# A two-layer graph network on one core: the queries as seven block products, the softmax sums through a small DRAM table, the first layer norm in pairs of tiles

## The chip, the core and the metric

The kernel runs on one core of a Trainium2 chip. A core has TensorE (PE, matrix products into PSUM, with its weight loads shown as PEld), VectorE (DVE), ScalarE (ACT), GpSimd (POOL) and SyncE (SP, which only issues DMAs here). Each engine works through its own queue of instructions in order and waits for the others by semaphores. The metric is the device time of the whole kernel in microseconds, the median of several runs. All arithmetic is in float32.

## What is computed

There are B = 16 graphs of N = 1024 nodes with C = 256 channels; they share one adjacency matrix. The first layer mixes nodes by attention whose queries come from a weighted adjacency, the second is a graph convolution with two batch norms.

```python
# layer 0
h  = relu(layernorm(x))
c  = mean(h, axis=2)                                   # one number per node
A  = |(|sigmoid(c_j - c_i) - 0.5| - 0.5)| * 2          # symmetric
g  = relu((h^T @ (adj * A)) * para)                    # C x N, the queries
k, v = split(h @ kv_w)
x  = x + softmax(g_heads @ k^T * scale) @ v            # 4 heads of 64
# layer 1
h  = relu(layernorm(x))
An = adj + I;  dinv = rsqrt(rowsums + colsums - diagonal)
agg = (dinv_i * An_ij * dinv_j) @ h
y  = batchnorm(relu(batchnorm(agg @ W1^T + b1)) @ W2^T + b2)
x  = x + y
```

## The kernel before

A tile has 128 partitions. A graph has eight tiles of nodes (NT = 8) and two chunks of 128 channels (CC = 2); FB = 512 nodes is a half of the nodes[...]. The four heads are held as two channel chunks k with two heads each, so one *unit* of attention is (graph b, chunk k, half of the nodes f): 64 units.

The function `layers(False)` does everything up to the hidden layer of the second part; `layers(True)` and `second("s")` are a fallback that is skipped when the watched sums are in range. `second("f")` does the rest: hidden activations back from DRAM, batch norm, the product with W2, batch norm, residual.

**The foreground.** `attention()` (L806) walks 256 steps: each step is a quarter of a unit, two key tiles. `scores` (L696) makes four score products and two exponentials, `Unit.add` (L725) adds the exponentials up on VectorE in `acc`, `Unit.values` (L736) multiplies the previous step's exponentials with `v`. When a unit is through, `divide` (L756) sums `acc` over partitions by a product with ones (L762), takes 128x512 reciprocals in four pieces (L771), multiplies the output with them (L774), keeps their extremes (L777, L778), and two steps later `finish` (L792) transposes the output and adds it to `x` (L802).

**The background.** Between `values` and the next step's scores, `attention` draws *pieces* of about 1.7 us of TensorE from a generator, `background(b)` (L612), until the share that is due is done. The background of graph b prepares others: the weighted adjacency of graph b+1 (`weigh`, L363: abs and tanh on ScalarE, times adj on VectorE), its queries (`queries`, L407), its keys and values (`keys_values`, L441), the second layer norm of graph b-1, its aggregation over the graph (`aggregate`, L489) and hidden layer (`hidden`, L549), and for graph b+2 the norm, the broadcast of its node means (`differences`) and its transposes (`transposed`). `weave` runs several generators side by side, `soon` puts an action behind the next piece, and the marker `TOP` has a piece run between a step's scores and its values. Thus the program order, not a scheduler, decides what stands behind what on each engine.

**Queries before.** For each half q of the columns, two PSUM banks take the sum over eight node tiles: 16 pieces of four small matmuls per graph, 64 instructions and 128 records in a trace (a float32 matmul leaves two). The weights `w` live in four buffers.

**Aggregation.** It is already a block scheme of seven products instead of eight over 2x2 blocks (Strassen's idea in Winograd's form), with the blocks of the scaled adjacency made once by `graph()` (L221) during graph 1 and read from DRAM (`aht_d`) for each graph, three pieces ahead. Degrees are taken by `degrees()` (L203) during graph 0, from a second reading of the transposed adjacency.

**DMA queues.** SP issues all loads in program order: x, adj, para, aht, and the second layer's `yin` (L973). POOL issues the writes: x1, `y_d` (L565) from four `y` buffers, `aht_d`.

The first lines of the kernel's own order:

```python
norm = Norm(0, True)
run(norm.all())
differences(0, columns_of(csums[0], "c0"))
for k in range(CC):
    transposed(0, k)
run(weave(keys_values(0), (8 - AHEAD, islice(weighers[0], AHEAD))))
```

Of the kernel before, what the change touches and what calls it, by code (L numbers as in the profile page):

```python
# [17 lines left out]
P = 128  # L18
# [5 lines left out]
def gnn_two_layers_kernel(  # L24
# [36 lines left out]
    w2 = const.tile([P, HC, C], F32, name="w2")  # L61
# [4 lines left out]
    stats2 = const.tile([P, CC, B * NH, 6], F32, name="stats2")  # L66
# [6 lines left out]


# [10 lines left out]
    def layers(shifted):  # L85
# [12 lines left out]
        p3 = st.enter_context(tc.tile_pool(name=f"p3_{kind}", bufs=3))  # L98
        p4 = st.enter_context(tc.tile_pool(name=f"p4_{kind}", bufs=4))
# [41 lines left out]

        def bank(name):
            return ps_mm.tile([P, FB], F32, tag="mm", name=name)
# [15 lines left out]
        def load_adj(q, th, name):  # L159
            t = p4.tile([P, TH, FB], F32, tag="adj", name=name)  # L160
            nc.sync.dma_start(
                out=t,
                in_=adj[th * TH * P : (th + 1) * TH * P, q * FB : (q + 1) * FB].rearrange(
                    "(t p) m -> p t m", p=P
                ),
            )
            return t
# [4 lines left out]
        dbc = big.tile([P, N], F32, name="dbc")  # L172
        w1 = big.tile([P, CC, H1], F32, name="w1")
        rows = big.tile([P, NH, NT], F32, name="rows")

        def columns_of(col, name):

            cbs = []
            for g in range(NT // 4):
                cb = p2.tile([P, 4, P], F32, tag="cb", name=f"cb_{name}_{g}")  # L180
                nc.vector.tensor_copy(
                    cb, col[:, 4 * g : 4 * g + 4].unsqueeze(2).to_broadcast([P, 4, P])
                )
                cbs.append(cb)
# [10 lines left out]
        def load_adj_t(t, name):  # L195
            tile_ = p4.tile([P, N], F32, tag="adj", name=f"{name}_{t}")
# [3 lines left out]
        deg_sm = big.tile([P, 6, NT], F32, name="deg")  # L200
        row, diag, col, deg, tmp_deg, dinv = (deg_sm[:, i, :] for i in range(6))

        def degrees():  # L203

            nc.sync.dma_start(out=w1, in_=w1_t.rearrange("(k p) j -> p k j", p=P))
            nc.sync.dma_start(out=w2, in_=w2_t.rearrange("(k p) c -> p k c", p=P))
            nc.vector.tensor_reduce(row, rows.rearrange("p q t -> p t q"), AX.X, ALU.add)
            for t in range(NT):
                a = load_adj_t(t, "at")
                yield 0.0  # L210
                blk = a[:, t * P : (t + 1) * P]
                nc.scalar.activation(a, a, AF.Copy, accum_out=col[:, t : t + 1])
                db = p1.tile([P, P], F32, tag="db", name=f"db_{t}")
                nc.vector.tensor_mul(db, blk, ident)
                nc.vector.tensor_reduce(diag[:, t : t + 1], db, AX.X, ALU.add)
                yield 0.0
            nc.vector.tensor_add(deg, col, row)
            nc.vector.tensor_sub(deg, deg, diag)
            rsqrt(dinv, deg, 1.0, tmp_deg)

        def graph():  # L221


            HT, HB = NT // 2, FB // 2
            for t in range(HT):
                for part in range(2):
                    cols = slice(part * HB, (part + 1) * HB)
                    a = p4.tile([P, 2, NH, HB], F32, tag="adj", name=f"au_{t}_{part}")
# [6 lines left out]
                    for n in range(2):  # L235
                        if part == t * P // HB:
                            blk = a[:, n, n, t * P % HB : t * P % HB + P]
                            nc.vector.tensor_add(blk, blk, ident)
                        nc.vector.tensor_mul(
                            a[:, n], a[:, n], dbc.rearrange("p (m c) -> p m c", m=NH)[:, :, cols]  # L240
                        )
# [12 lines left out]
                    yield 0.0  # L254

# [87 lines left out]
        def transposed(b, k):  # L343

            h = hs["a", b]
            ht = p3.tile([P, N], F32, tag="ht", name=f"ht_{b}_{k}")
            hts.setdefault(b, []).append(ht)
            for g in range(NH):
# [14 lines left out]
        def weigh(b):  # L363
# [11 lines left out]
            for slot in range(2 * NH * NP + 1):  # L375
# [11 lines left out]
                if not odd and i < NH * NP:  # L387
# [3 lines left out]
                    w = p4.tile([P, TH, FB], F32, tag="w", name=f"w_{b}_{q}_{th}")  # L391
# [14 lines left out]

        def queries(b):  # L407

# [32 lines left out]
        def keys_values(b):  # L441
            ht = hts[b]
            ks[b] = [p4.tile([P, N], F32, tag="k", name=f"k_{b}_{k}") for k in range(CC)]
            for j in range(CC):
                for g in range(NH):
# [28 lines left out]
        def quarters(b):  # L474


            h = hs["b", b]
            HT = NT // 2
            return [h[:, n * HT : (n + 1) * HT, c * P : (c + 1) * P] for c in (0, 1) for n in (0, 1)]

        def combine(b):


            a11, a12, a21, a22 = quarters(b)
            s1s[b] = p1.tile([P, NT // 2, P], F32, tag="s1", name=f"s1_{b}")
            nc.vector.tensor_add(s1s[b], a21, a22)
            nc.vector.tensor_sub(a21, a11, a21)

        def aggregate(b):  # L489
# [5 lines left out]
            def load(upto):  # L495
                while len(pieces) <= min(upto, 7 * NP // 2 - 1):
                    i, th = divmod(len(pieces), NP // 2)
                    i = order[i]
                    a = p4.tile([P, TH, FB], F32, tag="adj", name=f"aht_{b}_{i}_{th}")
# [3 lines left out]
            load(2)  # L503
            yield 0.0
            a11, a12, a21, a22 = quarters(b)
            s1 = s1s[b]
# [4 lines left out]
            add, sub = nc.vector.tensor_add, nc.vector.tensor_sub  # L511

# [4 lines left out]
            def second(m):  # L517
                add(c11, m, c12)
                sub(a12, a12, a11)

            def fifth(m):
                add(c22, m, c21)
                add(c12, m, c12)

            for i, (left, after) in enumerate(
# [6 lines left out]
                    (a22, lambda m: add(c21, m, c21)),  # L532
                    (a12, lambda m: add(c12, m, c12)),
# [3 lines left out]
                for th in range(NP // 2):  # L537
                    n = i * NP // 2 + th
                    load(n + 3)
# [35 lines left out]
        def normed(b):  # L575
# [3 lines left out]
            combine(b)  # L579
# [4 lines left out]
        def normed_last():  # L584
# [6 lines left out]
            combine(B - 1)  # L591
            nc.gpsimd.dma_start(out=x1_d[B - 1], in_=xs[B - 1])

        def prepare(b, products):
# [8 lines left out]
            for k in range(CC):  # L603
                yield from weave(islice(products, 3), (0, islice(w, 3)))
# [7 lines left out]
        def background(b):  # L612

            nothing = iter(())
            if b == 0:
                yield from prepare(1, nothing)
                yield from weave(queries(1), (0, weighers[1]), (1, degrees()))
                cbs = columns_of(dinv, "deg")
                if B > 2:
                    load_x(2)  # L620
                    yield from weave(keys_values(1), (1, Norm(2, True).all()))
                else:
                    yield from keys_values(1)
# [3 lines left out]
                if B > 2:  # L627
                    yield from prepare(2, nothing)
# [3 lines left out]
            if b + 1 < B:  # L632
                whole = graph() if b == 1 else nothing
                yield from weave(queries(b + 1), (0, weighers[b + 1]), (0, whole))
                yield next(gather)
                yield from weave(keys_values(b + 1), (0, normed(b - 1)))
# [79 lines left out]
        class Unit:  # L716


            def __init__(self, b, k, f):
                self.at = (b, k, f)  # L720
                self.name = f"{b}_{k}_{f}"
                self.acc = None
                self.later = []
# [32 lines left out]
            def divide(self):  # L756

                b, k, f = self.at
                self.pt = ps_t.tile([P, FB], F32, tag="t", name=f"sums_{self.name}")
                for e in range(2):  # L760
                    r = slice(e * HD, (e + 1) * HD)
                    nc.tensor.matmul(  # L762
                        self.pt[r, :], ones, self.acc[:, e, :], start=True, stop=True
                    )
                self.inv = p1.tile([P, FB], F32, tag="inv", name=f"inv_{self.name}")
                u = (b * CC + k) * NH + f

                def invert(half):
                    for j in range(2 * half, 2 * half + 2):
                        c = slice(j * P, (j + 1) * P)  # L770
                        nc.vector.reciprocal(self.inv[:, c], self.pt[:, c])  # L771

# [437 lines left out]
```

## Time and profile before

| | us |
|---|---|
| median of three runs | 2698.32 (2697.36 to 2698.34) |
| the profiled execution | 2699.94, its span 2698.10 |
| head: first score product of attention | from 62 on |
| graphs 2 to 14, one period each | 148.26 |
| first layer's last hidden piece to the second layer's first product | 2418 to 2422 |
| second layer, end | 2422 to 2698 |

The granted TensorE clock is 0.988 on average over the span. The page's groups name line, engine, operation, output and inputs; "xN | busy, mean ns | idle before" follow. A float32 matmul of 128x64 weights on 512 columns shows a mean of 592 ns, but they overlap: what one costs is read from how long a run of them takes. The DMA table gives, per issue, size and median time to landing: `aht` 512 KB 4.2 us, `adj` 512 KB 4.2, `para` 256 KB 4.1, `y_d` 256 KB 2.8, `x_d` 1024 KB 4.2, `yin` 1024 KB 6.3, `xo` 512 KB 8.5.

### The profile page before, as it was taken

How to read it: one execution, taken by the hardware profiler on the slowest of the kernel's cores; microseconds unless marked ns; L12 is line 12 of the kernel's file. 1: busy time of each engine (PE TensorE's matmuls, PEld its weight loads, DVE VectorE, ACT ScalarE, POOL GpSimd, SP SyncE). 2: the span in 40 equal slices, each digit the busy share in tenths (PEclk: the TensorE clock that was granted, in tenths of full speed). 3: DMA queues.
4: the chain of work that ended last, by engine and by line, in shares of the span. 5: the costliest groups of instructions: out<-in, count | busy, mean ns of one | idle time of the engine just before them, and what ended most of it. 6: DMA issues, size and time to landing. Idle time of an engine off the chain costs nothing.

```text
span 2698.1 us, 32021 instructions
## 1 busy us (share of the span) xinstructions
PE 2620.7 (97%) x12106; PEld 968.3 (36%) x12106; DVE 1742.3 (65%) x2624; ACT 1292.3 (48%) x1845; POOL 363.2 (13%) x428
## 2 busy tenths in 40 slices
PE   7999999999999999999999999999999999989994
PEld 3333333333333333333333333333333333324443
DVE  5767666666666656666666666566666666656675
ACT  5653444536363544445363635444453634335544
POOL 0016000000000100000000001000000001026653
PEclk9999999999999999999999999999999999999997
DMA  4416414243332424142423324241424213355549
GB/s 156 159 58 225 161 53 164 86 148 103 107 116 98 141 80 158 51 168 83 150 100 109 114 98 141 84 155 51 168 82 152 99 63 118 113 215 187 202 182 364
DMA packets 128613, 355.05 MB, mean 132 GB/s; under 512 B 11969, under 2 KB 32961, under 8 KB 122305
## 3 DMA queue, kind: packets, MB, share of 16 engines
q1 hardware_dynamic: 109120, 278.44, 30.3%
q0 software_dynamic: 19328, 74.46, 7.3%
q8 instruction: 98, 1.61, 0.2%
q14 instruction: 67, 0.54, 0.1%
HBM read 278.41 MB, written 74.45 MB: 131 GB/s over the span
## 4 chain that ended last, share of the span: by engine, by line
PE 93%; DMA 3%; DVE 2%; issue 2%; ACT 1%; POOL 0%; SPq 0%; POOLq 0%; DVEq 0%; ACTq 0%
PE sc L704 18%; PE o L745 18%; PE pg L149 16%; PE pa L149 13%; PE py L149 7%; PE m_f L1017 7%; PE pk L149 4%; PE pv L149 4%; PE sums L762 2%; DMA out_dram<-xo_f 2%; PE ot L798 1%; PE htp L352 1%; PE cbp_c L192 1%; DMA y_d<-y 0%; DVE acc L734 0%
## 5 line engine op out<-in xcount | busy, mean ns | idle before, releaser
L712 ACT ACTIVATE p<-sc 128x1024 f32<-128x1024 f32 x512 | 496.4, 1021 | 700.8 <-PE sc L704 700.6
L734 DVE TENSOR_TENSOR acc<-acc,p 128x1024 f32<-128x1024 f32 x384 | 471.2, 1227 | 133.8 <-ACT p L712 112.5
L704 PE MATMUL sc<-q,k 64*128 64x512 f32 x2048 | 510.6, 617 | 0.5 <-ACT p L712 0.5
L745 PE MATMUL o<-p,v 128*64 128x512 f32 x2048 | 496.1, 605 | 0.0
L149 PE MATMUL pg<-w,h_a 128*64 128x512 f32 x2048 | 457.1, 596 | 7.5 <-DVE q L432 7.5
L149 PE MATMUL pa<-aht,h_b 128*64 128x512 f32 x1536 | 346.0, 592 | 2.7 <-DMA aht<-aht_d 2.7
L704 PEld LDWEIGHTS sc<-q,k 64*128 64x128 f32 x2048 | 176.6, 186 | 321.9 <-issue 270.3
L149 PEld LDWEIGHTS pg<-w,h_a 128*64 128x64 f32 x2048 | 148.2, 138 | 301.8 <-issue 281.7
L771 DVE RECIPROCAL inv<-sums 128x128 f32<-128x128 f32 x256 | 223.7, 921 | 24.6 <-PE sums L762 24.6
L149 PE MATMUL py<-at,w 128*64 128x512 f32 x1024 | 230.8, 592 | 2.1 <-ACT y L564 2.1
L745 PEld LDWEIGHTS o<-p,v 128*64 128x64 f32 x2048 | 124.3, 136 | 286.1 <-issue 285.9
L394 ACT ACTIVATE w<-cbc,csum 128x512 f32<-128x512 f32 x256 | 170.2, 714 | 74.3 <-PE pg L149 74.2
L731 DVE TENSOR_TENSOR acc<-p,p 128x1024 f32<-128x1024 f32 x64 | 78.5, 1226 | 194.8 <-ACT p L712 194.8
L381 DVE SCALAR_TENSOR_TENSOR w<-w,adj 128x1024 f32<-128x1024 f32 x128 | 156.5, 1223 | 54.7 <-ACT w L402 54.7
L149 PEld LDWEIGHTS pa<-aht,h_b 128*64 128x64 f32 x1536 | 110.6, 137 | 216.6 <-issue 204.9
L564 ACT ACTIVATE y<-py,vec 128x512 f32<-128x512 f32 x128 | 87.6, 684 | 188.4 <-PE py L149 155.1
L565 POOL DMA_DIRECT2D y_d<-y x128 | 70.7, 553 | 685.1 <-ACT y L564 681.9
L402 ACT ACTIVATE w<-w 128x1024 f32<-128x1024 f32 x128 | 134.8, 1053 | 1.7
L149 PEld LDWEIGHTS py<-at,w 128*64 128x64 f32 x1024 | 74.0, 137 | 147.8 <-issue 131.3
L149 PE MATMUL pv<-kvw,ht 128*64 128x256 f32 x1024 | 116.2, 379 | 0.4 <-DVE v L469 0.4
L82 POOL TENSOR_SCALAR lnsm_b<-mv_b 128x4 f32<-128x4 f32 x32 | 7.3, 230 | 805.2 <-DVE mv_b L277 805.1
L802 DVE TENSOR_TENSOR x<-ot,x 128x512 f32<-128x512 f32 x64 | 44.2, 691 | 110.6 <-PE ot L798 109.8
(133 smaller groups left out, 2526.4 us busy)
## 6 DMA issues: line engine op xcount, KB each, us to landing
aht<-aht_d SPq DMA_DIRECT2D x224, 512.0 KB, 4.2
adj<-in_adj_dram SPq DMA_DIRECT2D x128, 512.0 KB, 4.2
y_d<-y POOLq DMA_DIRECT2D x128, 256.0 KB, 2.8
yin_f<-y_d SPq DMA_DIRECT2D x32, 1024.0 KB, 6.3
x<-in_x_dram SPq DMA_DIRECT2D x32, 512.0 KB, 4.7
para<-in_para_dram SPq DMA_DIRECT2D x64, 256.0 KB, 4.1
x_d<-x POOLq DMA_DIRECT2D x16, 1024.0 KB, 4.2
xo_f<-x_d SPq DMA_DIRECT2D x32, 512.0 KB, 8.5
```

The lines of the kernel that those rows point to most:

```text
L149: nc.tensor.matmul(dst[r], left[:, r], right, start=start, stop=stop)
L381: nc.vector.scalar_tensor_tensor(w, w, 1.0, a, op0=ALU.add, op1=ALU.mult)
L394: nc.scalar.activation(w[:, t, :], cbc[:, q * FB : (q + 1) * FB], AF.Abs, bias=csum[:, th * TH + t : th * TH + t + 1], scale=-1.0,)
L402: nc.scalar.activation(made[i], made[i], AF.Tanh, scale=-0.5 / C)
L564: nc.scalar.activation(y, made, AF.Identity, bias=b1[:, j : j + 1])
L704: nc.tensor.matmul(sc[:, e, :], ks[b][k][r, m * P : (m + 1) * P], qs[b][k][r, f * FB : (f + 1) * FB], start=True, stop=True,)
L712: nc.scalar.activation(pr, sc, AF.Exp)
L731: nc.vector.tensor_add(self.acc, self.held, pr)
L734: nc.vector.tensor_add(self.acc, self.acc, pr)
L745: nc.tensor.matmul(self.o[r, :], vs[b][k][:, m, r], pr[:, e, :], start=(m == 0), stop=(m == NT - 1),)
L771: nc.vector.reciprocal(self.inv[:, c], self.pt[:, c])
L1017: nc.tensor.matmul(made, left[:, j, :], right[:, j, :], start=(j == 0), stop=(j == JH - 1))
```

## The change

1. *Queries.* From graph 2 on, `queries` computes the product of h^T with the weighted adjacency in 2x2 blocks by the same seven-product scheme as `aggregate`: `combine` makes sums and differences of the blocks of h, `take` subtracts blocks of `w` from each other on VectorE between the products, and each product's result is added into the query tile from PSUM. Graphs 0 and 1 keep the old form (`plain_queries`). All eight `w` tiles of a graph now have buffers (`p8`), which `aggregate` shares for its pieces, loading five ahead; adj tiles have three buffers, not four.
2. *Order.* In the background of graph b the four key products come before the queries, with four slots of weights beside them, then two slots per piece (`double`); the norm of graph b-1 starts at the tenth piece of the queries; the value products follow.
3. *Sums.* A row of sums is copied from PSUM by ScalarE, written to a DRAM table by POOL, and read back transposed as a 128x8 tile; `add_output` takes the reciprocal of that, multiplies the transposed output from PSUM with it and adds it to x.
4. *Adjacency.* `degrees` reads each tile of the transposed adjacency once, takes the sums and the diagonal, and makes the unscaled blocks; `graph` is gone. The column scaling moves to the outputs of `aggregate` (`scale`), four multiplications by `dbc` per graph.
5. *Start.* Graph 0's first norm goes tile pair by tile pair; the first half of the nodes is transposed and its keys are made before the second half's transposes and the broadcast of the means. x of graph 2 is loaded with that of graph 1.
6. *W2.* `w2` and `stats2` move from the constants into the second layer's pool; `w2` is loaded at its start.

```diff
+        def combine(tag, b, engine):
+            a11, a12, a21, a22 = quarters(tag, b)
+            s1s[tag, b] = p1.tile([P, NT // 2, P], F32, tag="s1", name=f"s1_{tag}_{b}")
+            engine.tensor_add(s1s[tag, b], a21, a22)
+            engine.tensor_sub(a21, a11, a21)
...
+            def take(i, x, y, part):
+                nc.vector.tensor_sub(block(i)[part], block(x)[part], block(y)[part])
+            def first(m):
+                nc.scalar.copy(c12, m)
+                nc.scalar.copy(c21, m)
+                nc.vector.tensor_sub(a11, s1, a11)
+            def second(m):
+                add(c11, m, c12)
+                nc.vector.tensor_sub(a12, a12, a11)
+                soon(lambda: finish(0, 0))
+            def third(m):
+                add(c22, m, c21)
+                take(2, 3, 2, 0)
+                load_para(0, 1)
...
+            def sixth(m):
+                for c in (c12, c22, c21):
+                    add(c, m, c)
...
+                    (a11, 0, (), first),
+                    (a12, 1, ((0, 2, 0, 0), (0, 2, 0, 1)), second),
+                    (s1, 0, (), third),
+                    (a12, 3, ((2, 3, 2, 1), (0, 3, 0, 0)), fourth),
+                    (a21, 2, ((0, 3, 0, 1), (1, 1, 0, 0)), fifth),
+                    (a11, 0, ((1, 1, 0, 1),), sixth),
+                    (a22, 1, (), seventh),
...
+                w, products, norm = weighers[b + 1], keys_values(b + 1), normed(b - 1)
+                yield from weave(islice(products, 4), (0, islice(w, 4)))
+                yield from weave(queries(b + 1), (0, double(w)), (9, islice(norm, 5)))
                 yield next(gather)
-                yield from weave(keys_values(b + 1), (0, normed(b - 1)))
+                yield from weave(products, (0, norm))
...
+            def sums(self):
...
+                row = py.tile([P, FB], F32, tag="y", name=f"row_{self.name}")
+                nc.scalar.copy(row, pt)
+                nc.gpsimd.dma_start(
+                    out=sums_d[u], in_=row.rearrange("(e r) c -> e r c", r=HD)[:, 0, :]
+                )
+                self.inv = p2.tile([P, FB // P, 2], F32, tag="inv", name=f"inv_{self.name}")
+                for e in range(2):
+                    nc.gpsimd.dma_start(
+                        out=self.inv[:, :, e], in_=sums_d[u][e].rearrange("(j q) -> q j", q=P)
                     )
...
+            def add_output(self):
...
+                nc.vector.reciprocal(self.inv, self.inv)
+                nc.vector.tensor_mul(
+                    self.os.rearrange("p (j e c) -> p j e c", j=J, e=2),
+                    pt.rearrange("p (j e c) -> p j e c", j=J, e=2),
+                    self.inv.unsqueeze(3).to_broadcast([P, J, 2, HD]),
+                )
...
+            def scale(c, g):
+                nc.vector.tensor_mul(c, c, dbc[:, g * FB : (g + 1) * FB])
...
-                    a = p4.tile([P, TH, FB], F32, tag="adj", name=f"aht_{b}_{i}_{th}")
+                    a = p8.tile([P, TH, FB], F32, tag="w", name=f"aht_{b}_{i}_{th}")
...
         with st:
+            w2 = wp.tile([P, HC, C], F32, name="w2")
+            nc.sync.dma_start(out=w2, in_=w2_t.rearrange("(k p) c -> p k c", p=P))
```

## The prediction

> **What bounds the kernel now.** I read the page's busy shares first, then the chain of work that ended last, then windows over single stretches, then the groups.
>
> ```profile
> PE 2620.7 (97%) x12106; PEld 968.3 (36%) x12106; DVE 1742.3 (65%) x2624; ACT 1292.3 (48%) x1845; POOL 363.2 (13%) x428
> ...
> PE 93%; DMA 3%; DVE 2%; issue 2%; ACT 1%; POOL 0%; SPq 0%; POOLq 0%; DVEq 0%; ACTq 0%
> ```
>
> TensorE is busy 97% and is 93% of the chain: the only engine whose work decides. The windows say where that isn't so (columns: length, then PE, PEld, DVE, ACT, POOL busy with counts, granted clock, DMA share, GB/s).
>
> ```profile
> 641.56:789.82 148.26, 148.26 (x714) 52.91 (x712) 95.37 (x143) 71.20 (x104) 10.06 (x17) 1.00 0.34 114
> 186.68:345.02 158.34, 151.95 (x714) 53.26 (x712) 112.80 (x167) 71.30 (x104) 59.98 (x73) 0.97 0.53 180
> ...
> 170.00:180.00 10.00, 5.59 (x34) 3.58 (x30) 6.00 (x9) 7.80 (x13) 0.00 (x0) 0.87 0.11 37
> 180.00:190.00 10.00, 10.00 (x38) 3.28 (x40) 5.40 (x7) 5.66 (x7) 0.00 (x0) 0.79 0.22 71
> ...
> 210.00:220.00 10.00, 5.05 (x12) 1.30 (x14) 8.09 (x10) 3.25 (x5) 7.36 (x8) 0.57 0.66 213
> ```
>
> The first line is one graph's period in the steady part: 148.26 us, TensorE busy in all of it, VectorE idle for 53 us. The second is the same stretch of graph 1, when `graph()` builds the adjacency blocks: 158.34 us, 10.1 us longer. The others show two stalls, each followed by a lower clock.
>
> ```profile
> L149 PE MATMUL pg<-w,h_a 128*64 128x512 f32 x2048 | 457.1, 596 | 7.5 <-DVE q L432 7.5
> L771 DVE RECIPROCAL inv<-sums 128x128 f32<-128x128 f32 x256 | 223.7, 921 | 24.6 <-PE sums L762 24.6
> ...
> L777 DVE TENSOR_REDUCE seen<-inv 128x1 f32<-128x512 f32 x64 | 42.8, 669 | 0.0
> ...
> 641.56 6.87 PE pg L149 x32
> ...
> 2401.12 2.01 SPq L973 DMA_DIRECT2D yin_f<-y_d  x4
> ```
>
> `pg` is 128 records per graph; the chain has 32 of them in 6.87 us, 0.2147 us each. The last line, from the timeline, shows that the second layer's inputs are requested at 2401, before the first layer's last products are written.
>
> [...] No run here shows 4-byte pieces.
>
> **The change part by part.**
>
> *Queries as seven products.* Graphs 2 to 15, 14 of them: 16 products of a quarter become 14, so 112 instead of 128 records. 14 x 16 x 0.2147 = 48.1 us of TensorE less.
>
> *VectorE's bill for it.* Per graph added: two combinations, two updates of h, eight subtractions of weights (128x1024, 1.227), nine additions from PSUM: 13 x 0.69 + 8 x 1.227 = 18.8 us. Scaling by `dbc`: 4 x 0.69 = 2.8. Removed: sixteen reciprocals (14.7) and most of eight reductions (5.4, about 1.4 stays). Net about +3, so over a period it fits: some 98 of 145 us. But it is not spread evenly. I followed the three queues by hand through the five steps (a step is four scores, four values and about 2.5 pieces) that hold the seven products: VectorE has 45 us of work there beside 47 of TensorE.
> - First tight place: the third product reads `w[0]` after a subtraction. Ahead of it stand two acc additions, and their exponentials stand behind ScalarE's abs and tanh for the last weights (1.33 + 1.06), which now run two slots a piece. Exponentials end about 6.3 us into the step, two additions and the subtraction about 8.8 to 9.2; TensorE gets there at 8.0. Wait 0.8 to 1.2.
> - Second: after the seventh product VectorE has its addition, three multiplications by para, norm's leftovers, the output's two operations and two acc additions ahead of the copies of `v`. The third `pv` wants a bank of PSUM at 46.8 us, the copies free it between 47.2 and 48.3. Wait 0.4 to 1.5.
> Instructions that follow each other independently start up to 0.1 us sooner than their durations say (the trace has 0.69 us additions 0.61 apart), which makes the low ends. I take 1.6 us a graph, 22.4 in all; bounds 0 (the lags absorb each other) and 3.4 (every wait longer by half a microsecond to one).
>
> *Sums by GpSimd.* The two sum matmuls stay. A ScalarE copy (0.586) joins, hidden: ScalarE has 76 us of idle a graph. Then three DMAs on POOL: a write, and two reads of 512 four-byte pieces that wait for the write. Behind these POOL has `y_d` writes and rsqrt. Chain: copies 1.2, issue 0.55, landing 2.8, two issues of 0.8 (the 512-piece `aht_d` row), landing between 2.8 and 8.5 (fastest and slowest medians of the DMA table; I take `para`'s 4.1): 10.3 us, at most 14.7. The output is wanted two steps later, 16.7 us by TensorE's order. Hidden, cost 0. The four `y` buffers also hold the row: a write held back 6 us still lands before its buffer's turn four pieces later (11 us). A later landing is the slow rival below.
>
> *Degrees and blocks in one pass, scaling moved to the outputs.* Graph 1 loses the whole of `graph()`: its 10.1 us go. Graph 0 gets the POOL work (50 us) in its place, with three adj buffers instead of four, but no longer ends in transposes that have nothing beside them (the stall at 170 to 190 us, 4.4 of idle plus about 2 of low clock): `v` products now lie between. POOL is full for four steps, so I leave graph 0 a stall of about 4 us. Sum -12; bounds -18 and -2.
>
> *Head.* Norm in pairs: h of the first half at about 10.2 us instead of 11.2, and keys need no broadcast before them, so `pk` starts near 12 rather than 18.39. Two broadcasts and four transposes (about 3 us) come between. Attention starts some 3.5 us sooner; bounds 0 and 6. Cover: adj's fourth tile now waits for a buffer and x of graphs 1 and 2 stands behind it on SP, needed only from 37 us on.
>
> *Tail.* `w2` is loaded inside the second layer into memory that the `y` tiles held; by the program's waits its DMA starts after the last `y_d` write has landed, and the four `yin` loads stand behind it on SP. Before, they started at 2401 and slowed those writes. Now: deeper prefetch of `aht` saves the 3 us TensorE waits there, the `y` writes flow at TensorE's pace (3.4 us), the last lands 14 us later than `yin` was requested. Then 0.5 + 1 + 1 MB at about 300 GB/s (the rate at 2400 to 2420)[...]: the second `yin` at 2427, the first product of both halves at 2430.5 instead of 2426.1. Cost 4; bounds 0 and 9.
>
> **Sum.** -48.1 + 22.4 - 12 - 3.5 + 4 = -37.2 us. The profiled execution has a span of 2698.10 us and took 2699.94; the median is 2698.32, within 0.1%, so I subtract from the median: 2661.
>
> **The rivals.**
> - *The whole cut lands.* VectorE's lag never reaches TensorE: 2661 - 22 = 2639. For it: 53 us of idle VectorE a period, and `pa`, built alike, waits 2.7 us in all. Against it: `pa` has no weights being made beside it.
> - *VectorE eats the queries' gain.* 3.4 us a graph: 2661 + 14 x 1.83 = 2687, still faster by the rest. For it: 45 of 47 us.
> - *Slower: the small reads come late.* Place: VectorE's reciprocal of `inv`, which stands ahead of the acc additions. If reads land in 12 us instead of 4, the chain takes 18.2 and VectorE stands 1.5 us at each of 64 units; about 0.7 reaches TensorE: +45, 2706. It decides from a landing of about 11.9 us, where 0.58 us a unit gives back the 37. For it: 1024 pieces of 4 bytes a unit, 65,536 in all, against 128,613 packets in the whole run now. Against it: DMA is busy a third of the period.
> - *It doesn't do what it says.* In the program's order the products' line has 112 matmuls less, 224 records, so only a wait could take the cut away: the cases above. 2698 where they balance.
>
> **How the numbers follow.** Forecast 0.61, whole cut 0.20, eaten gain 0.10, slower 0.06, nothing 0.03. Time 2661. The range reaches from the whole cut with a little more at graphs 0 and 1 to just past the eaten gain: 2635 to 2690. Measured from no change by 0.2% (5.4 us, what a measurement of this kernel can tell): faster 0.88 (the first three, less a part of the eaten gain with a bad start and end), same 0.05, slower 0.07.
>
> **What would show it.** Right: a period of about 146.4 us with `pg` at 112 records; 1.0 to 2.5 us of TensorE idle a graph, put down to `w` subtractions or `v` copies; graph 1 as long as the others; reciprocals of eight elements with no wait on `inv`; the `yin` loads issued near 2380, some 18 us after the last `pa`. Wrong: a period of 144.8 (no stall), or 148 with VectorE near full in the queries; VectorE waiting for a DMA of `inv`; a stall over 8 us in graph 0; or `m_f` starting where the rest of the sum would have put it.

## The result and the profile after

The changed kernel takes 2699.28 us (2698.89 to 2700.18, 4 runs), beside 2697.84 us (2696.56 to 2698.34, 4 runs) for the kernel before on the same chip: a ratio of 1.0007, 95% interval 0.9989 to 1.0024. Nothing that can be told from no change. The forecast was 2661. The profiled execution has a span of 2697.0 us.

The page, busy shares first and then the engines' shares of the chain that ended last:

```profile
PE 2579.3 (96%) x11882; PEld 953.2 (35%) x11882; DVE 1742.1 (65%) x2777; ACT 1338.3 (50%) x1953; POOL 547.1 (20%) x624
...
PE 79%; DVE 7%; ACT 4%; DMA 4%; issue 3%; POOL 2%; SPq 0%; POOLq 0%; DVEq 0%; ACTq 0%
```

TensorE has the 224 records less that the change takes out and is busy for 41.4 us less (2620.7 before) in a span that is 1.1 us shorter. So some 40 us of work became 40 us of idle time, and the chain, 93% TensorE before, now runs for 21% through other engines. Windows of the changed kernel say where (length, then PE, PEld, DVE, ACT, POOL busy, clock, DMA share, GB/s): graph 1, which took 158.34 us before, a steady graph, and 120 us of graph 0.

```profile
227.90:374.68 146.78, 145.28 (x699) 51.92 (x696) 98.19 (x158) 74.11 (x109) 22.41 (x29) 1.00 0.34 115
...
481.30:628.08 146.78, 145.27 (x698) 51.88 (x697) 98.20 (x156) 74.09 (x110) 22.58 (x30) 1.00 0.34 115
...
60.00:180.00 120.00, 88.43 (x366) 29.23 (x364) 56.04 (x93) 61.48 (x108) 49.12 (x61) 0.87 0.40 129
```

The last stretch in the kernel before:

```profile
60.00:180.00 120.00, 114.67 (x564) 43.60 (x560) 83.68 (x126) 78.54 (x116) 4.44 (x6) 0.99 0.31 107
```

The steady period is 146.78 us, 1.48 less than before, and graph 1 is now as long as any other. Graph 0 is where the gain went: in the same 120 us TensorE gets through 366 records instead of 564, idle for 31.6 us and at a clock of 0.87. What it waited for, over the whole changed kernel (total, times, longest):

```profile
PE sc L827 <- ACT p L835: 29.0, 5, 14.0
PE m_f L1145 <- ACT yin_f L1107: 10.8, 1, 10.8
PE pv L155 <- DVE v L584: 10.6, 14, 0.8
PE pg L155 <- DVE w L457: 9.3, 13, 0.7
```

The second line is the start of the second layer, the last two are one short wait each in nearly every graph. The four long waits of the first line lie between 100 and 154 us: score products wait for a PSUM buffer that an exponential has still to empty. ScalarE is not full there (61 of 120 us). What it stood at, and what SP stood at, between 60 and 185 us:

```profile
ACT au_f L228 <- DMA au_f<-in_adj_t_dram: 27.0, 7, 7.2
...
SPq L167 <- DMA aht_d<-au_f: 43.0, 4, 12.4
SPq L222 <- DMA aht_d<-au_f: 35.5, 4, 11.8
```

One round of it in the timeline of the changed kernel (start, duration, engine and line, with the idle time before in brackets):

```profile
95.75 1.21 SPq L222 DMA_DIRECT2D au_f<-in_adj_t_dram  x2
...
98.79 0.63 ACT L228 ACTIVATE au_f<-au_f 128x512 f32<-128x512 f32 x1 [6.40 <-DMA au_f<-in_adj_t_dram]
...
102.73 0.83 POOL L246 DMA_DIRECT2D aht_d<-au_f  x1
...
107.91 1.21 SPq L222 DMA_DIRECT2D au_f<-in_adj_t_dram  x2
...
111.02 0.63 ACT L228 ACTIVATE au_f<-au_f 128x512 f32<-128x512 f32 x1 [7.15 <-DMA au_f<-in_adj_t_dram]
...
113.82 1.91 ACT L835 ACTIVATE p<-sc 128x1024 f32<-128x1024 f32 x2
...
114.87 3.79 PE L827 MATMUL sc<-q,k 64*128 64x512 f32 x8 [14.04 <-ACT p L835]
```

Read from the top: a piece of the adjacency is asked for, lands, is summed by ScalarE, is subtracted by GpSimd, and its blocks are written. SP asks for the next piece at 107.91, 12.2 us after the last: the 512 KB write issued at 102.73 has then just landed, after 5.1 us, and the wait list puts SP's waits on these writes. ScalarE, done with everything ahead of it, stands 7.15 us at the next accumulation, which needs that piece; the exponentials for which TensorE waits stand behind it, and start at 113.82. The write shown is the second of the eight; their median is 3.4, and the next round, with 3.5 us for it, is no shorter (SP asks again at 120.45). So it is not a slow write that makes the round: the landing is simply part of it.

The three sum DMAs gave no trouble. The changed kernel's DMA table (last number: median us to landing) and the group of the small reciprocals:

```profile
inv<-sums_d POOLq DMA_DIRECT2D x128, 2.0 KB, 2.6
...
L911 DVE RECIPROCAL inv<-inv 128x8 f32<-128x8 f32 x64 | 12.4, 193 | 6.3 <-DMA inv<-sums_d 6.3
```

And the end of the first layer, from the timeline:

```profile
2411.53 0.38 SPq L1078 DMA_DIRECT2D w<-in_w_t_dram  x1
2411.96 20.41 SPq L1101 DMA_DIRECT2D yin_f<-y_d  x6
...
2418.80 3.75 PE L1145 MATMUL m_f<-yin_f,w 128*128 128x512 f32 x4 [10.76 <-ACT yin_f L1107]
```

### The profile page after: what moved, and what is told of

The parts are those of the page before. It is cut to its first block, busy times and chain, and to the rows that moved or that the text cites. A ratio compares the mean times of both kernels' runs of the same rounds, so it can differ in the third digit from the quotient of the medians.

```text
span 2697.0 us, 32235 instructions
## 1 busy us (share of the span) xinstructions
PE 2579.3 (96%) x11882; PEld 953.2 (35%) x11882; DVE 1742.1 (65%) x2777; ACT 1338.3 (50%) x1953; POOL 547.1 (20%) x624
## 2 busy tenths in 40 slices
DMA packets 133606, 351.39 MB, mean 130 GB/s; under 512 B 17856, under 2 KB 38848, under 8 KB 127296
## 3 DMA queue, kind: packets, MB, share of 16 engines
q0 software_dynamic: 25472, 75.00, 8.5%
## 4 chain that ended last, share of the span: by engine, by line
PE 79%; DVE 7%; ACT 4%; DMA 4%; issue 3%; POOL 2%; SPq 0%; POOLq 0%; DVEq 0%; ACTq 0%
PE sc L827 16%; PE o L868 16%; PE pa L155 13%; PE pg L155 9%; PE py L155 8%; PE m_f L1145 7%; PE pk L155 4%; PE pv L155 2%; PE sums L885 2%; DMA out_dram<-xo_f 2%; DVE acc L857 2%; ACT w L395 1%; PE htp L353 1%; ACT w L403 1%; DVE q L484 1%
## 5 line engine op out<-in xcount | busy, mean ns | idle before, releaser
L155 PE MATMUL pg<-w,h_a 128*64 128x512 f32 x1600 | 359.7, 595 | 3.9 <-ACT k L567 2.1
L888 POOL DMA_DIRECT2D sums_d<-row x64 | 37.2, 582 | 1051.0 <-ACT row L887 1051.0
L155 PEld LDWEIGHTS pg<-w,h_a 128*64 128x64 f32 x1600 | 115.8, 138 | 233.5 <-issue 212.4
L457 DVE TENSOR_TENSOR w<-w,w 128x1024 f32<-128x1024 f32 x112 | 131.4, 1214 | 0.0
L155 PE MATMUL pv<-kvw,ht 128*64 128x256 f32 x1024 | 119.2, 380 | 10.6 <-DVE v L584 10.6
L893 POOL DMA_DIRECT2D inv<-sums_d x128 | 98.2, 770 | 137.6 <-DMA sums_d<-row 93.1
L681 DVE BATCH_NORM_STATS2 stats<-y 128x6 f32<-128x512 f32 x128 | 85.7, 687 | 61.5 <-ACT y L677 59.6
```

The costliest lines, as they stand in the source:

```text
L155: nc.tensor.matmul(dst[r], left[:, r], right, start=start, stop=stop)
L457: nc.vector.tensor_sub(block(i)[part], block(x)[part], block(y)[part])
L893: nc.gpsimd.dma_start(out=self.inv[:, :, e], in_=sums_d[u][e].rearrange("(j q) -> q j", q=P))
```

## The experiments

Below, "graph 0" is the distance between the first broadcast products of graph 1's node means and those of graph 2's: 105.25 us before (66.81 to 172.06), 135.03 in the changed kernel (65.55 to 200.58). "Graph 1" is the next such distance: 143.29 and 133.94. Where no range is given, a kernel was run once; the kernel before lay between 2696.2 and 2700.1 us in all its runs beside these kernels.

The two distances of graph 0 do not hold the same work, as the TensorE records in their windows show (before, then changed):

```profile
66.81:172.06 105.25, 104.60 (x513) 38.57 (x513) 76.63 (x117) 66.94 (x100) 4.44 (x6) 1.00 0.33 110
...
65.55:200.58 135.03, 104.38 (x456) 36.41 (x457) 64.09 (x105) 67.66 (x117) 57.57 (x71) 0.89 0.39 125
```

In the new order 32 records of value products, 16 of `o` and 8 of scores come behind the second mark, in graph 1. A run of them takes 0.11, 0.22 and 0.24 us a record, so that is about 9 us. By this estimate graph 0 would take some 96 us in the changed kernel if nothing were lost. What it loses is then about 39 us, not the difference of 29.8, and the forecasts of some 105 us that follow were made from a distance that holds more work.

### The pass over the adjacency in buffers of its own

```diff
+            spare = (dbc viewed as [P, 2, NH, HB], w1 viewed so)
...
-                    a = p3.tile([P, 2, NH, HB], F32, tag="adj", ...)
+                    a = spare[part]
...
+            nc.sync.dma_start(out=w1, ...)      # moved behind the pass
```

> The pass over the adjacency in graph 0 reads its pieces into two buffers of its own (the memory of dbc and w1, which nothing uses before the pass ends; w1 is loaded behind the pass) instead of the ring of three that it shares with the weights' pieces. Theory A: the 30 us lost in graph 0 come from that ring. A piece's load waits until an earlier piece's write-back has landed, so that a piece takes 12.5 us, and ScalarE's accumulation of that piece stands ahead of the exponentials. Then TensorE's idle time ahead of sc between 60 and 180 us falls from 29.0 to under 8, the distance between the broadcasts of the differences of graphs 1 and 2 from 135.0 to 104 to 112, and the whole is 2668 to 2678 us. Theory B: the amount of work (32 us of GpSimd's subtractions, 10 of accumulations, all in graph 0) takes the time; the ring only shows it. Then the distance stays above 125 and the whole above 2688.

Measured: 2677.01 us (2675.53 to 2678.82), 0.9921 of before (0.9905 to 0.9938); graph 0 112.09 us, graph 1 133.96, steady period 146.80. Waits of TensorE and the window of graph 0 in this kernel:

```profile
PE sc L831 <- ACT p L839: 8.6, 3, 5.1
...
60.00:180.00 120.00, 107.91 (x492) 38.35 (x490) 69.17 (x111) 73.55 (x124) 60.18 (x71) 0.94 0.43 142
```

The same work, GpSimd even busier in the window, and 22.9 of the 39 us of graph 0 are back. The amount of work alone (theory B: above 125) is not the cause of these; the buffers are. The edit takes the pieces out of the ring and also adds two buffers; a ring of four was not tried, so which of the two helps is open. The residue was a little more than I allowed: 8.6 us of idle time, not under 8, and 112.09 at the edge of the range. Of the 39 us some 16 are still lost. Part of it is the same round, now of two buffers: ScalarE waits 10.3 us for pieces here.

### The accumulations left out

```diff
-                        nc.scalar.activation(a[:, n], a[:, n], AF.Copy, accum_out=...)
+            nc.vector.memset(col, 4.0); nc.vector.memset(col_2, 4.0)
```

> The sixteen accumulations by ScalarE that give the columns' sums are left out (the sums are set to a constant, so the degrees are wrong); loads, VectorE's diagonal, GpSimd's subtractions and the writes stay, and the ring of three stays. Theory A with ScalarE's queue as the carrier: the loads are as late as before, but no exponential stands behind them; idle ahead of sc falls from 29.0 to under 8 us and the whole is 2668 to 2680. If the late loads hold TensorE by another way (VectorE's diagonal ahead of the acc additions, the weights' pieces behind the loads on SP), the idle time moves to that releaser and the whole stays above 2688.

Measured: 2683.81 us, graph 0 116.27. Waits in this kernel between 60 and 185 us:

```profile
PE sc L826 <- ACT p L834: 9.3, 2, 8.9
...
ACT row L886 <- issue: 10.4, 1, 10.4
```

Between the two forecasts. With the ring as it was, taking the waiting instruction out of ScalarE's queue brings 18.8 of the 39 us: ScalarE's order carries about half of the loss. (It also takes away 13.0 us of ScalarE's work; ScalarE was busy for only 61 of 120 us.) The longest wait that is left, 8.9 us, is behind a copy of a row of sums on which ScalarE stood for 10.4 us. The profile names no releaser, but the order of time points to one:

```profile
108.92 0.29 DVE L233 TENSOR_TENSOR db<-au_f,ident 128x128 f32<-128x128 f32 x1 [4.84 <-DMA au_f<-in_adj_t_dram]
109.24 0.29 DVE L234 TENSOR_REDUCE deg<-db 128x1 f32<-128x128 f32 x1
...
109.61 0.59 ACT L886 COPY row<-sums 128x512 f32<-128x512 f32 x1 [10.35 <-issue]
```

The row takes one of the four `y` buffers, and so does the diagonal block `db` of a piece. The copy starts 0.08 us after VectorE is through with such a block, and VectorE had waited for the piece. So here too a late load is the likely holder, by way of a second shared ring; it wasn't tried.

### Two passes again

```diff
-    one pass: load, sums, diagonal, add I, subtractions, writes   (graph 0)
+    degrees(): load, sums, diagonal                               (graph 0)
+    graph(): load, add I, subtractions, writes                    (beside graph 1's queries)
```

> One part undone: degrees in graph 0 and blocks in graph 1 are two passes again, as before the change, with nothing written back in graph 0; all else is the changed kernel's. My prediction's step was that one pass is 12 us better than two. Theory A: graph 0 comes down to some 105 us between the broadcasts of differences 1 and 2, graph 1 up by 8 to 11, the whole is 2676 to 2684: two passes are 15 to 23 us better than one as it stands. Rival: graph 0's loss has to do with the new order of keys, transposes and norm there and not with the pass; then graph 0 stays above 125 and the whole is above 2699.

Measured: 2693.89 us (2692.31 to 2695.28), 0.9984 of before (0.9978 to 0.9991). Graph 0 fell to 109.12, toward the 105 of theory A, but graph 1 rose by 19.1 to 153.02, not by 8 to 11, and the whole missed the range. Waits of TensorE in graph 1, and lines of its timeline:

```profile
PE pv L155 <- DVE v L588: 7.3, 1, 7.3
PE pv L155 <- DVE q L494: 5.8, 1, 5.8
PE pg L155 <- DVE w L461: 2.7, 1, 2.7
...
252.65 1.04 POOL L82 TENSOR_TENSOR lnsm_b<-lnsm_b,neg_half 128x4 f32<-128x4 f32 x1
253.73 0.16 DVE L288 TENSOR_TENSOR lnsm_b<-lnsm_b,deg 128x4 f32<-128x4 f32 x1 [7.75 <-POOL lnsm_b L82]
258.24 3.68 PE L155 MATMUL pv<-kvw,ht 128*64 128x256 f32 x16 [5.83 <-DVE q L494]
```

SP waits for the write-backs here too (25.6 us), but TensorE is held by another path. GpSimd has the small operations of the second norm in the same queue as the subtractions of the pass, its block writes and the DMAs of the sums; VectorE waits for that norm (7.75 and 3.50 us), and its results for the value products come late. So in graph 1 it is GpSimd's queue that carries the loss, and theory A does not cover it. In graph 0 nothing is written back, and ScalarE still waits 9.0 us for the adjacency and some 13 us are lost by the estimate of 96. SP asks late there for another reason: it waits for VectorE, up to 5.0 us at a time, which still has to read the tiles of the ring. One pass or two makes 5.4 us in all.

### Plain queries

```diff
-                yield from weave(queries(b + 1), (0, double(w)), ...)
+                yield from weave(plain_queries(b + 1), (0, double(w)), ...)
```

> One part undone: queries of graphs 2 to 15 as sixteen plain products again (the weights still made two slots a piece), all else the changed kernel's. The prediction's step says 3.44 us of TensorE a graph more and 1.6 us of waiting less. With what the trace shows (period 146.78, of which 144.83 is work if nothing waited) it is 3.44 more and 1.95 less: period 148.2 to 148.4, the whole 2718 to 2722. If the seven products brought nothing, the period stays at 146.8 and the whole at 2699.

Measured: 2722.43 us, period 148.27 (148.26 to 148.27), as expected, and the whole just above its range. The seven products are worth 1.49 us a graph in the kernel as it stands. Not in graph 15: the changed kernel shows no wait of VectorE's lag behind 2090 us, so there they bring all of their 3.44, and 13 x 1.49 + 3.44 is 22.8 of the 23.2 us that this kernel is slower than the changed one.

### The two short waits, and both

```diff
-                    nc.vector.tensor_copy(vs[b][k]..., pv...)      # e5: v copied by ScalarE
+                    nc.scalar.copy(vs[b][k]..., pv...)
...
             def first(m):                                          # e6: one piece earlier
                 ...
+                take(0, 2, 0, 0)
...
-                    (a12, 1, ((0, 2, 0, 0), (0, 2, 0, 1)), second),
+                    (a12, 1, ((0, 2, 0, 1),), second),
```

> The copies of v out of PSUM go to ScalarE instead of VectorE, all else the changed kernel's. The trace puts 0.76 us a graph of TensorE's idle time on pv waiting for v, my second tight place (I took 0.4 to 1.5). If VectorE's late copies are that wait, the period falls from 146.78 by 0.6 to 0.9 to 145.9 to 146.2 and the whole by 9 to 13. If ScalarE then delays the exponentials by its 16 copies a graph, the wait moves to sc or to the third product and the period stays within 0.2 of 146.78 or grows.

> The subtraction that makes the third product's first weights is put on VectorE one piece earlier (behind the first product instead of midway in the second), all else the changed kernel's. The trace puts 0.72 us a graph of idle time on it, my first tight place (I took 0.8 to 1.2). If VectorE's lag behind TensorE is the cause, the period falls by 0.5 to 0.75 to 146.0 to 146.3. If it comes because its inputs are made late (ScalarE's tanh and the multiplication of w[4]), the wait stays or grows, and the acc additions behind it come later too: 146.7 or more.

Measured: with `v` on ScalarE 2686.53 us, period 145.78; with the subtraction earlier 2689.04 us, period 145.85. Each wait is gone from its kernel's list and the other one stays as it was, 9.4 and 10.8 us in all: two independent lags of VectorE, worth 1.00 and 0.93 us a graph, a little more than forecast and some 30% more than the idle time that the list puts on them. That is 0.78 and 0.72 us in each of the 13 graphs that have them (of the 10.6 us for `v`, 0.4 is a wait at 28.9 us, before attention starts, and no part of the lag).

The third edit puts the `yin` loads ahead of `w2`'s on SP:

```diff
+            for i in range(4):
+                load_y(i)
             w2 = wp.tile([P, HC, C], F32, name="w2")
             nc.sync.dma_start(out=w2, ...)
```

> The second layer's first four yin loads are put ahead of w2's load on SP, all else the changed kernel's. The trace has 10.8 us between the end of the last py and the first m_f, where the kernel before has 4.8. Theory: the wait of w2's load for the last y writes holds the yin loads behind it. Then the yin land before the last py ends, w2 lands some 3 us after its issue at 2411.5, the gap is 6 to 8 us and the whole 2695 to 2697. If the early yin loads collide with the y writes and the last aht loads, the gap stays at 10 or py gets waits of its own: 2699 or more.

Measured: 2695.34 us; `yin` is asked for at 2380.72, the gap before the first `m_f` is 7.4 us and ends with `w2`'s landing. As expected.

All four edits together:

> The changed kernel with the pass's own two buffers, v copied by ScalarE, the one subtraction earlier and yin ahead of w2. If the terms are independent: 2677 less 0.7 + 0.65 for each of 14 graphs (19) and less 3 at the end: 2652 to 2660. If VectorE's and ScalarE's queues only pass the waiting on to the next instruction, the period stays above 146.3 and the whole above 2668.

Measured: 2644.98 us (2643.22 to 2645.92), 0.9801 of before (0.9783 to 0.9819). It is below my range, which used the list's times for the two waits and 3 us for the end. With the measured ones, over the 13 graphs that have the lag, the terms give 2677.0 - 13 x 1.93 - 3.9 = 2648.0; graph 0 and the head bring another 1.5 us. So the terms are nearly independent. A steady graph of it:

```profile
453.76:598.59 144.83, 144.83 (x698) 51.77 (x697) 95.34 (x148) 76.31 (x118) 22.13 (x30) 1.00 0.35 117
```

TensorE is busy in all of the period, which is 3.43 us under the plain queries' 148.27. That is the whole cut that the prediction's first term counts.

### Loads one piece further ahead

The combined version, with this edit in outline:

```diff
+            fetch(piece 0); fetch(piece 1)
             for each piece n:
                 sums, diagonal, subtractions, writes of n
+                yield; fetch(piece n + 2); yield
```

> The combined version, and in the pass over the adjacency each load is put one piece further ahead of the accumulation that reads it (three slots of the background between them instead of one); the same work, the same two buffers. ScalarE waited 10.9 us for these loads in the combined version (6.8 and 4.1), and TensorE 7.9 us at sc for its exponentials. If these waits are the accumulations standing ahead of the exponentials, they go: distance between the broadcasts of the differences of graphs 1 and 2 from 110.9 to 102 to 106, the whole 2636 to 2640. If the write-backs set the pace whatever the order (two buffers, 12 us for each to come round), the distance stays within 2 us of 110.9 and the whole at 2643 to 2646.

Measured: 2643.67 us, graph 0 109.26 (110.89 and 108.89 in two kernels without this edit). ScalarE's waits between 60 and 180 us in this kernel:

```profile
ACT w L238 <- DMA w<-in_adj_t_dram: 7.0, 4, 2.8
ACT dbc L238 <- DMA dbc<-in_adj_t_dram: 4.0, 4, 2.8
```

The hope was missed and the other forecast came: 11.0 us of waiting where the combined version has 10.9, in eight waits of at most 2.8 instead of three with up to 5.1. Asking earlier in the program did not help here, since the buffers came free late: SP waits 41.7 us for the write-backs of the two.

### w2 in a pool of its own

```diff
+        w2p = st.enter_context(tc.tile_pool(name=f"w2p_{kind}", bufs=1))
...
-            w2 = wp.tile([P, HC, C], F32, name="w2")
+            w2 = w2p.tile([P, HC, C], F32, name="w2")
```

> The combined version, and w2 in a pool of its own that is opened ahead of the second layer's other tiles, so that its memory is only that of kvw and its neighbours and its load waits for the last py product instead of the last y writes. The gap between the last py and the first m_f was 10.8 in the changed kernel and 7.5 in the combined version, where it ended with w2's landing. Theory: it becomes 4.5 to 6, limited by the scales that need the last y's statistics, and the whole falls by 1.5 to 3 to 2642 to 2643.5. Rival: the write of y by GpSimd and the load collide and the gap stays at 7: 2645.

Measured: 2645.70 us (2644.52 to 2646.93), 0.9809 of before (0.9792 to 0.9825): no better than the combined version, and the gap is 8.2 us. `w2` is now asked for at 2356.4, right with the last py product, and lands 4.4 us later, but GpSimd stands at the scales of the second layer:

```profile
2361.88 0.23 POOL L81 TENSOR_SCALAR sm<-mv 128x2 f32<-128x2 f32 x1 [3.96 <-DMA y_d<-y]
```

This wait was there in the combined version too, with 2.32 us. Their tile, it seems, also lies in memory that the `y` tiles held. It is longer here: the last `y` write, now beside the load of `w2`, takes 4.0 us to land, where it takes 2.3 in the changed kernel. That fits the collision which the expectation named as the rival, with its 2645.

### Sums on VectorE as before

```diff
-    row copied by ScalarE, written to DRAM and read back as 128x8; reciprocal of 128x8
+    nc.vector.reciprocal(self.inv[:, c], self.pt[:, c])     # 4 x 128x128 a unit
+    nc.vector.tensor_mul(self.os, self.os, self.inv); two reductions of 128x512
```

> One part undone: the sums stay in PSUM and VectorE takes sixteen reciprocals of 128x128 a graph of them and scales with them, as before the change (their result in one of the y buffers); all else the changed kernel's. The prediction's step gave the new way a cost of 0 and counted VectorE's 14.7 us of reciprocals and some 4 us of reductions as removed. If that relief is what keeps VectorE's lag in the seven products small, the period grows from 146.78 by 1 to 4 us a graph and the whole to 2713 to 2755. If VectorE's idle time takes them in anyway (they stand where the units end, and only some units end inside the products), the period stays within 0.4 us of 146.8 and the whole within 6 us of 2699.

Measured: 2739.07 us, period 150.19 to 150.23. The page's busy shares, TensorE's waits, and a steady graph:

```profile
PE 2597.5 (95%) x11882; PEld 960.4 (35%) x11882; DVE 1999.8 (73%) x2969; ACT 1302.3 (48%) x1889; POOL 412.1 (15%) x432
...
PE pv L155 <- DVE v L584: 36.3, 14, 2.8
...
485.30:635.51 150.21, 146.73 (x698) 52.52 (x697) 114.42 (x169) 71.85 (x106) 14.02 (x17) 0.99 0.33 113
```

VectorE is far from full at 73%, and yet each graph is 3.41 us longer. The wait is the second tight place, `v` copies late behind VectorE's burst: 2.8 us a graph instead of 0.78 (2.0 more). The rest is in the same 698 records, which take 146.73 us instead of 145.27, at a clock of 0.99. With VectorE's old sums the seven products are slower (150.19) than the plain queries are with the new ones (148.27), or than they were with the old ones in the kernel before (148.26).

## Why the prediction was wrong, step by step

Distances between marks in the two profiles, without the working of the terms:

| term | predicted | measured |
|---|---|---|
| queries, work taken from TensorE, 14 graphs | -48.1 | -48.2 (148.27 less 144.83, times 14) |
| VectorE's lag in them | +22.4 | +25.4 (146.78 less 144.83, times 13: graph 15 shows none) |
| graphs 0 and 1, without the queries | -12 | +21.9 (see below) |
| head, to the first broadcast of graph 1's means | -3.5 | -1.3 (66.81 to 65.55) |
| tail, from graph 15's broadcast to `m_f`, without the queries | +4 | -1.3 (327.62 to 322.90, and 3.44 of that is the queries') |
| second layer, `m_f` to the end | 0 | +2.3 (275.9 to 278.2) |
| sum | -37.2 | -1.2 |

For graphs 0 and 1: from graph 1's broadcast to graph 3's it was 248.54 us and is 268.97, 20.4 more; one set of queries in it, with its lag, is 1.49 less, so 21.9. Both ends of this stretch stand at the same point of the program, so the work in it is the same but for the queries.

- *The step that failed* is "POOL is full for four steps, so I leave graph 0 a stall of about 4 us. Sum -12; bounds -18 and -2." The term that was off is that stall: graph 1's 10.1 us and the stall with its low clock (6.4: 4.4 of idle, and 2 estimated from the 0.79 of 180 to 190 us) did go, so +21.9 leaves some 38 us for graph 0 where I took 4; the estimate from the records above gives 39. I priced the pass by GpSimd's amount of work. GpSimd is busy for 49 of 120 us there and not the limit. What I left out is the round of a buffer: load, accumulate, subtract, write, landing of the write, 12.2 us, and eight pieces in turn through a ring that I had noted as "three adj buffers instead of four"; and that the accumulations put the end of that round at the head of ScalarE's queue. In its place the runs showed: with two buffers outside the ring 22.3 us of the whole are back, with the accumulations gone 15.5. The first is over half of the loss; some 13 us or more of it remain in every kernel that was run, and of these no run shows the whole cause. That two passes would be worse by 12 is wrong as well; with the rest of the new order they are 5.4 better (2699.28 less 2693.89).
- The other half of that step held: graph 1's `graph()` of 10.1 us is gone, and its stretch is 146.78 like the rest. The sign given there, "a stall over 8 us in graph 0", is what came.
- *VectorE's lag* was right in its two places, its releasers and nearly its size: 1.95 us in each of 13 graphs, where I took 1.6 in 14, within 0 and 3.4. The durations behind the 1.6 are in the trace before: 691 ns for `x` plus `ot` of 128x512 (L802), 1227 for `acc` plus `p` of 128x1024 (L734). The new subtractions of `w`, 128x1024 too, take 1214. Forecast: 146.4; measured: 146.78.
- *Sums*: cost 0 was right. Landing was 2.6 us where I took 4.1, and VectorE waited 6.3 us for `inv` in the whole run. The rival of late small reads is out. What spoke for it, 65,536 pieces against 128,613 packets, did not come either: the trace has 133,606 packets, and on GpSimd's queue 25,472 instead of 19,328, which is 96 more for the three DMAs of a unit. The same step undercounted the benefit: I summed VectorE's load per graph and found that it "fits", but the relief carries 3.41 us a graph, since it lies at the end of the queries where VectorE is late.
- *Head*: `pk` starts at 11.23 us, as forecast near 12 and 7.2 earlier than before. The other transposes and the broadcast between its two halves take 3.9 us (15.70 to 19.63), the first half itself 1.0 more than before, so the value products start 2.2 us earlier; 0.9 more goes in graph 0's queries. Of the 1.3 us that are left little can be said: in the twelve kernels with the new start the mark lies between 65.02 and 67.08 us, and before, in one profile, at 66.81.
- *Tail*: the order was right (`yin` issued 18 us behind the last `pa`, the gap 10.8 instead of 4.8 us), the sum was too dear: 5.9 us for the gap, and the waits of `pa`, `py` and `ot` of 6.2 us in all are gone, with 1 us more that I can't place. Before, five `y_d` writes beside the early `yin` loads took 6.2 to 9.4 us to land; in the changed kernel the last eight have a median of 2.3. ScalarE takes up the second `yin` at 2420.28, 8.75 us after `w2` was asked for; the forecast's 12 us or so for that were my estimate, in which only the 300 GB/s comes from the trace. The 2.3 us at the very end, in the last writes of the output, stay open.

## What to carry to other kernels

Where a tile is loaded, changed and written back, count the landing of the write into its buffer's round: here that is a median of 3.4 of some 12 us. Divide the number of pieces by the buffers that are free for them and multiply by that round before believing that work on an idle engine is free. Then look at which instruction waits for the load, and on whose queue: here an accumulation ahead of exponentials turned a late load of a side job into idle time of the engine that sets the end (29.0 us ahead of `sc`, 8.6 with the pass in buffers of its own). And a change of several parts has to be priced by where each part's work lies: the reciprocals were small in the sum over a graph and large at the one place where VectorE was late. Two marks can be compared only if the same work lies between them; the count of records tells.

## What was unexpected of the hardware

- Reads that the program writes as 512 pieces of 4 bytes, issued by GpSimd, land in 2.6 us in the median and 5.5 at most, no slower than a plain write of 256 KB from the same queue (`y_d`, 2.6). They do not show as 512 packets: two of them, from 121.6 us on, have 64 on GpSimd's queue.

```profile
q0 software_dynamic: 64, 0.00, 2.4%
...
inv<-sums_d POOLq DMA_DIRECT2D x2, 2.0 KB, 4.5
```

- The two short waits cost more than the list of waits says: they are listed with 0.78 and 0.72 us a graph, and their removal brought 1.00 and 0.93. The difference is in TensorE's own records: the same 698 of a graph have 145.27 us of busy time with the waits and 144.83 without, both at a clock shown as 1.00. Why they get longer wasn't settled; the ends of matmuls are modelled in the profile, but the periods do get shorter by the whole amount.
- A reciprocal of 128x8 on VectorE takes 193 ns where 128x128 took 921, so the transposed table makes sixteen reciprocals of a graph, 14.7 us, into four of 0.8 in all.
